# A four-layer graph network on one core: layer 2's table rows come from VectorE products, and its variances, deviations and messages go in two halves

## The chip, the cores and the metric

The kernel runs on one core of a Trainium2 chip. The core has five engines with instruction queues of their own: TensorE (PE in the profile, its weight loads PEld), VectorE (DVE), ScalarE (ACT), GpSimd (POOL) and SyncE (SP), which issues all DMAs here. The engines meet only through semaphores. The metric is the device time of one launch in microseconds. The kernel before takes 3417.18 us, the median of three runs (3413.88 to 3422.05).

## The reference

There are 64 independent graphs of 256 nodes with 128 features, and a sparse 256 x 256 weight matrix `adj` for each. Four layers follow one another; each first normalises its input and cuts it at zero, and adds its result to its input. The change lies in layer 2, which forms a message for every pair of nodes:

```
h   = relu(layernorm(x))
pre[i, j] = h[j] @ W1[:D] + h[i] @ W1[D:] + b1
msg[i, j] = gelu(layernorm(pre[i, j], g1, be1))
agg[i]    = sum over j of adj[i, j] * msg[i, j]
x = x + layernorm(concat(h, agg) @ W2 + b2, g2, be2)
```

Most entries of `adj` are zero, so most messages need not be formed.

## The kernel before

**Blocks and lanes.** A graph's 256 targets i are cut into 8 blocks of 32 (`NIB`, `IB`), its 256 sources j into 3 blocks of 86 (`NJB`, `JB`), which gives 24 blocks (`NT`). In each block the nonzero entries are numbered into at most 128 lanes (`CAP`). For each block t a one-hot matrix `hot[:, t, :]` of 128 rows and 128 lanes is made: rows 0 to 85 choose the source of the lane, row 86 (`JB`) is left for something else, rows 96 to 127 choose the target (`ROWS` is 96). A matmul of `hot[:, t, :]` with a matrix that holds a row for each source and each target then gives, for every lane, the sum of its source's row and its target's row.

**Two such matrices.** `entries` holds for every block the adjacency, the products and the squared lengths that make up the variances; `table` holds `near` (the sources' rows, already multiplied by g1, with b1g = b1 * g1 added) in rows 0 to 85 and `far` (the targets' rows) in rows 96 to 127. Row 86 of `table` is be1, and row 86 of `hot` gets the standard deviation of each lane, so that the matmul gives d * g1 + std * be1; multiplied by 1/std this is the normalised message. W1 and b1 have had their mean taken off in the setup, so the rows need none taken off.

**Layer 2 of one graph**, the generator `layer2` (L1122), in its order:

- `turned`, `near_squares` (L1147), `far_squares` (L1160): TensorE multiplies h by W1's halves into PSUM; ScalarE squares and sums the rows of the result (`a2`, `c2`). Then the graph passes from part "layer2" to "pairs".
- `sums` and `far` fill `entries`; `adjacent` (L1225) copies the adjacency into it by DMA, 96 rows per source block.
- Four groups `entries_of` (L1273) of six blocks each (`TE`): 24 matmuls of `hot` and `entries`; VectorE forms the weights `wgt` and the variances `var`.
- Beside them run `diagonal` (L1173, the messages of a node to itself, two chunks of 128 nodes in one bank), `sources` (L1186) and `targets` (L1208). These multiply h once more, now by `w1g` = W1 * g1, add b1g on VectorE (`near`) or copy on ScalarE (`far`), wait until the messages of the graph before have read the table (`gathered`), and fill the table: three DMAs from `near`, four from `far`.
- Then, once for all 24 blocks: VectorE clamps the variances; ScalarE takes Ln, then Exp twice, for the deviations `std` and their inverses `rs`; TensorE transposes `std`, ScalarE copies it (`stdT`), and a DMA writes it into row 86 of `hot` (L1311).
- Six `block_sums(c, j)` (L1329), the source block j outside and the half c of the targets inside: four matmuls of `hot` and `table`, a VectorE product with `rs`, Gelu on ScalarE, four matmuls that sum the messages by target in the PSUM tile `pagg`. `own_messages` does the same for the diagonal.

**The order of the work.** All layers of all graphs are Python generators, and a planner (`run`, L1453) steps them one at a time. Its `Clock` holds an assumed cost for every instruction and DMA, the time at which each engine comes free, and the last writers and readers of every tile. Among the steps that could begin soonest it takes the one most overdue: graph n is due at 53 us times n (`PERIOD`), less the time that the rest of a graph has taken from that point. Each engine receives its instructions in the order so chosen, so one changed step can move those behind it. Switching ScalarE between the function set that has Ln and Exp and the one that has Gelu and Tanh costs a preload (L117 in the profile), and the planner holds such a step back by 1 us (`SETL`). The dictionary `behind` says how many graphs may stand in each part. `together` and `begun` start several generators beside one another. Where TensorE's queue would be empty for long, `keep_warm` (L180) adds matmuls into an unused half of `pagg` (L189 in the profile). Nearly all other instructions have L267, the planner's issuing line.

**The start.** Lines 423 to 645 hold the setup. `products` (L466) forms `b1g` and `w1g` among others. The generator `fold`, which uses the table's room and is due before everything else, multiplies layer 3's weights; only after its last step may graph 0's table be filled. All loads stand in SyncE's queue in the order of the program.

Of the kernel before, what the change touches and what calls it, by code (L numbers as in the profile page):

```python
# [9 lines left out]
AF = mybir.ActivationFunctionType  # L10
ALU = mybir.AluOpType
AX = mybir.AxisListType
# [12 lines left out]
ROWS = P - IB  # L25
NT = NIB * NJB
NF = NC * NJB
# [244 lines left out]
class Sparse:  # L272
# [150 lines left out]
    def setup(self):  # L423
# [3 lines left out]
        self.ones = self.full("ones", [P, P], 1.0)  # L427
# [151 lines left out]
    def setup_lanes(self):  # L579
# [7 lines left out]
        for c in range(NC):  # L587
# [8 lines left out]
        lane1 = self.c("lane1", [P, CAP])  # L596
        incl = lane1
        nc.gpsimd.affine_select(
            out=incl, in_=self.ones, pattern=[[1, P]], compare_op=ALU.is_ge, fill=0.0, base=0, channel_multiplier=-1
# [20 lines left out]
        nc.gpsimd.iota(lane1, [[1, CAP]], base=1, channel_multiplier=0, **iota)  # L620
        nc.vector.memset(lane1[P - IB :], 1.0)
# [16 lines left out]
        self.near = self.c("near", [ROWS, NJB, D])  # L638
        nc.gpsimd.memset(self.near, 0.0)
        be1 = self.w["L2_gnn_be1"].rearrange("(o n d) -> o n d", o=1, n=1).broadcast_to([1, NJB, D])  # L640
        nc.sync.dma_start(out=self.near[JB : JB + 1], in_=be1)
# [480 lines left out]
    def layer2(self, n, g):  # L1122
# [9 lines left out]
        t2 = self.t("t2", [P, N])  # L1132
        a2 = self.t("a2", [P, NJB])
        c2 = self.t("c2", [P, NC])
        var = self.t("var", [P, NT + NC])
        table, entries = self.table, self.entries

# [9 lines left out]
        def near_squares():  # L1147
# [5 lines left out]
            for j in range(NJB):  # L1153
                w = self.width(j)
                self.squares(a2[:w, j : j + 1], pa[:w, j, :])
                yield
            self.close(self.ps)
            yield

        def far_squares():  # L1160
# [8 lines left out]
            yield  # L1169
            self.close(self.ps)  # L1170
            yield

        def diagonal():  # L1173
            po = yield from self.bank(self.ps, (P, NC, D))
            for c in range(NC):
                self.mm(po[:, c, :], [(hT[:, c * P : (c + 1) * P], self.w1own)])
            yield
            nc.vector.tensor_tensor(own, po, self.over(self.b1, NC), ALU.add)
# [3 lines left out]
            for c in range(NC):  # L1182
                self.squares(var[:, NT + c : NT + c + 1], own[:, c, :])
                yield

        def sources():  # L1186
# [12 lines left out]
            yield  # L1199
            self.close(self.ps)  # L1200
            for j in range(NJB):
                while self.gathered[j] < NC * n or not self.folded:
                    yield
                near = a[:, j].rearrange("p (o d) -> p o d", o=1).to_broadcast([ROWS, NIB, D])
                nc.sync.dma_start(out=table[:ROWS, j], in_=near)
                yield

        def targets():  # L1208
            pc = yield from self.bank(self.ps, (P, NC, D))
            for c in range(NC):  # L1210
# [4 lines left out]
            yield  # L1215
            self.close(self.ps)
            while min(self.gathered) < NC * n or not self.folded:
                yield
            for q in range(NQ):
                of = self.over(far, NJB)[q * IB : (q + 1) * IB]  # L1220
# [4 lines left out]
        def adjacent():  # L1225
            while self.looked < NT // TE * n:
                yield
            for j in range(NJB):
                at, end = j * JB, min(j * JB + ROWS, N)
# [12 lines left out]
        yield from self.together(n, [turned(), near_squares(), far_squares()])  # L1242
        yield from self.enter(n, "layer2", "pairs")
# [29 lines left out]
        def entries_of(t0):  # L1273
# [14 lines left out]
            nc.vector.tensor_reduce(var[:, t0 : t0 + TE], own2, AX.X, ALU.add)  # L1288
            self.give("own2")
            yield  # L1290

        filled = self.begun(n, [sources(), targets()])
        yield from self.together(n, [entries_of(t0) for t0 in range(0, NT, TE)] + [diagonal()])
        rs = self.t("rs2", [P, NT + NC])
        nc.vector.tensor_scalar(rs, var, 0.0, D * LN_EPS, ALU.max, ALU.add)
        yield
        nc.scalar.activation(rs, rs, AF.Ln)
        yield
        std = self.t("std", [P, NT])
        nc.scalar.activation(std, rs[:, :NT], AF.Exp, scale=0.5)  # L1300
        yield
        nc.scalar.activation(rs, rs, AF.Exp, scale=-0.5)
        yield
        pt = yield from self.bank(self.ps, (P, P))
        nc.tensor.transpose(pt[:NT], std, self.ident)
        yield
        stdT = self.t("stdT", [NT, P])
        nc.scalar.copy(stdT, pt[:NT])
        yield
        self.close(self.ps)  # L1310
        nc.sync.dma_start(out=g.hot[JB : JB + 1], in_=stdT)  # L1311
        yield
# [5 lines left out]
        def own_messages():  # L1318
            for c in range(NC):
                nc.vector.scalar_tensor_tensor(  # L1320
                    own[:, c, :], own[:, c, :], rs[:, NT + c : NT + c + 1], self.g1, ALU.mult, ALU.mult
# [7 lines left out]
        def block_sums(c, j):  # L1329

            ts = [(c * NQ + q) * NJB + j for q in range(NQ)]
            yield from self.take("pre")
# [7 lines left out]
            yield from self.messages(pre, m, rs[:, ts[0] : ts[-1] + 1 : NJB])  # L1340
# [13 lines left out]
        yield from self.together(n, [block_sums(c, j) for j in range(NJB) for c in range(NC)] + [own_messages()])  # L1354
# [805 lines left out]
```

## Time and profile before

| | |
|---|---|
| median of 3 runs | 3417.18 us |
| profiled execution | 3408.92 us |
| its span, first to last instruction | 3407.1 us |
| mean granted TensorE clock | 0.971 |
| TensorE busy, keep-warm included | 3110.8 us, 91% |
| keep-warm matmuls | 2074, 291.7 us |
| VectorE busy | 2683.3 us, 79% |
| ScalarE busy | 2288.5 us, 67%; 350 function set loads of 1283 ns in it |
| GpSimd busy | 1317.3 us, 39% |
| one transpose of deviations per graph | first 126.3 us, last 3352.5 us |

Busy time is the union of an engine's instructions. TensorE's matmuls are pipelined and their ends are modelled, so the time between starts says more than the duration. The chain is followed back from the last instruction: at each step to what released it, or to the instruction before it on its engine. A line of groups gives the engine, the operation, the tiles written and read, the shapes, the count, then busy us and the mean ns of one, then the idle time in front of them and what ended it.

### The profile page before, as it was taken

To read this page: it belongs to the slowest core of one execution; us is meant where nothing else is said; L and a number is where in the kernel's file an instruction comes from. 1 tells how busy PE (TensorE), PEld (TensorE's weight loads), DVE (VectorE), ACT (ScalarE), POOL (GpSimd) and SP (SyncE) were. 2 spreads that over 40 slices of the span, in tenths; PEclk is the share of its full clock that TensorE was granted. 3 is DMA by queue.
4 is the path that set the end of the run, shared out by engine and by line. 5 is a ranking of instruction groups with operands and counts; after the bars stand their busy time and mean duration, and the time that the engine had idled before them with its cause. 6 is when DMAs were issued, how large, how long until landed. Compare 5 with 4: busy or idle time off the path is not lost.

```text
span 3407.1 us, 74541 instructions
## 1 busy us (share of the span) xinstructions
PE 3110.8 (91%) x26043; PEld 2717.1 (80%) x26043; DVE 2683.3 (79%) x9292; ACT 2288.5 (67%) x5983; POOL 1317.3 (39%) x3024
## 2 busy tenths in 40 slices
PE   5898999999999999999899999999999999999798
PEld 3687788888888788788787877887887878888687
DVE  8778888787878788887877788788878887786763
ACT  3676667767776677666666767776766776766562
POOL 3534444434433344333343434434433433443230
PEclk7899999999999999999999999999999999999899
DMA  1221112112212122112122121121211121121110
GB/s 48 59 50 47 40 47 58 48 42 52 53 38 55 34 55 58 39 48 53 34 54 58 33 58 44 43 58 48 56 40 49 38 58 48 39 56 42 37 48 25
DMA packets 387733, 161.02 MB, mean 47 GB/s; under 512 B 158739, under 2 KB 387350, under 8 KB 387350
## 3 DMA queue, kind: packets, MB, share of 16 engines
q1 hardware_dynamic: 387350, 156.18, 18.2%
q8 instruction: 208, 3.41, 0.4%
q14 instruction: 175, 1.43, 0.1%
HBM read 28.19 MB, written 8.39 MB: 11 GB/s over the span
## 4 chain that ended last, share of the span: by engine, by line
PE 56%; DVE 23%; ACT 14%; issue 4%; POOL 3%; DMA 1%; DVEq 0%; SPq 0%; ACTq 0%; POOLq 0%
PE bank L267 53%; ACT junka L267 3%; ACT L117 3%; DVE hot L267 2%; DVE agg L267 2%; DVE pos L267 2%; DVE lg L267 1%; ACT h L267 1%; PE pagg L267 1%; DVE rank L267 1%; ACT lg L267 1%; PE pagg L189 1%; DVE held L267 1%; DVE msg L267 1%; POOL lnrs L267 1%
## 5 line engine op out<-in xcount | busy, mean ns | idle before, releaser
L117 ACT ACT_TABLE_LOAD x350 | 449.1, 1283 | 5.8
L267 PE MATMUL bank<-table,hot 128*128 128x128 f32 x3072 | 377.0, 278 | 29.4 <-DMA hot<-stdT 11.6
L267 PEld LDWEIGHTS bank<-table,hot 128*128 128x128 f32 x3072 | 360.8, 193 | 44.8 <-issue 15.5
L267 PE MATMUL bank<-entries,hot 128*128 128x65 f32 x3072 | 358.6, 274 | 0.3 <-DVE near L267 0.2
L267 PEld LDWEIGHTS bank<-entries,hot 128*128 128x128 f32 x3072 | 356.6, 193 | 2.1 <-PE bank L267 0.3
L267 PE MATMUL bank<-wsd,f 128*128 128x256 f32 x1280 | 331.7, 390 | 25.2 <-ACT f L267 20.2
L267 DVE TENSOR_TENSOR msg<-bank,rs 128x512 f32<-128x512 f32 x384 | 256.6, 682 | 81.7 <-PE bank L267 78.9
L189 PE MATMUL pagg<-off,identb 128*128 128x256 bf16 x2074 | 291.7, 279 | 0.3 <-DVE agg L267 0.3
L267 ACT ACTIVATE msg<-msg 128x512 f32<-128x512 f32 x384 | 231.1, 625 | 87.7 <-DVE msg L267 85.7
L267 PEld LDWEIGHTS bank<-wsd,f 128*128 128x128 f32 x1280 | 232.4, 193 | 65.3 <-ACT f L267 32.7
L267 DVE TENSOR_TENSOR hot<-bank,lane 128x384 f32<-128x384 f32 x512 | 261.1, 545 | 18.7 <-PE bank L267 18.1
L267 DVE TENSOR_TENSOR sd<-bank,bsd 128x512 f32<-128x512 f32 x256 | 175.1, 684 | 111.8 <-PE bank L267 110.0
L267 ACT ACTIVATE h<-x,lnnb,lnrs 128x128 f32<-128x128 f32 x384 | 172.0, 485 | 123.6 <-DVE lnnb L267 118.5
L267 PE MATMUL bank<-adjT,sd 128*128 128x256 f32 x768 | 232.8, 385 | 2.7 <-DVE sd L267 2.3
L189 PEld LDWEIGHTS <-identb 128*128 128x128 bf16 x2074 | 202.3, 101 | 39.1 <-issue 2.7
L267 PE MATMUL bank<-adj,sd 128*128 128x256 f32 x768 | 229.9, 381 | 0.0
L267 POOL TENSOR_SCALAR lnrs<-lnmv 128x2 f32<-128x2 f32 x256 | 76.3, 298 | 339.1 <-DVE lnmv L267 304.3
L267 POOL TENSOR_TENSOR lnrs<-lnrs,mhalf 128x2 f32<-128x2 f32 x256 | 193.7, 757 | 21.3
L267 PEld LDWEIGHTS bank<-adjT,sd 128*128 128x128 f32 x768 | 146.0, 192 | 29.2 <-DVE sd L267 4.7
L267 PEld LDWEIGHTS bank<-adj,sd 128*128 128x128 f32 x768 | 147.4, 192 | 20.5
L267 PE MATMUL bank<-w,hT 128*128 128x128 f32 (+2 forms) x896 | 150.2, 286 | 2.8 <-ACT tgt L267 0.9
L267 POOL TENSOR_TENSOR adjT<-adjT,binv 128x512 f32<-128x512 f32 x64 | 83.1, 1299 | 178.4 <-ACT binv L267 173.3
(267 smaller groups left out, 8484.0 us busy)
## 6 DMA issues: line engine op xcount, KB each, us to landing
table<-near SPq DMA_DIRECT2D x192, 384.0 KB
table<-far SPq DMA_DIRECT2D x256, 96.0 KB
adj<-in_adj_dram SPq DMA_DIRECT2D x64, 256.0 KB
x<-in_x_dram SPq DMA_DIRECT2D x64, 128.0 KB
out_dram<-f SPq DMA_DIRECT2D x64, 128.0 KB
entries<-adjT SPq DMA_DIRECT2D x64, 96.0 KB
entries<-adjT SPq DMA_DIRECT2D x64, 84.0 KB
entries<-adjT SPq DMA_DIRECT2D x64, 54.0 KB
```

Source lines behind the costliest of these rows:

```text
L117: self.tc.keep_in_program_order(self.nc.scalar.preload_act_table_set(self.set))
L189: self.nc.tensor.matmul(out, lhsT=lhsT, rhs=rhs, start=False, stop=False, skip_group_check=True)
L267: return c.tc.keep_in_program_order(f(*args, **kw))
```

## The change

- `near_squares` multiplies its PSUM result by g1 on VectorE into `near`, in two operations, after the squares and before the bank is released; `far_squares` likewise into `away` (the tile `far`). The second multiplication of h and `w1g` are gone. `near` exists twice, for even and odd graphs, `far` too.
- The bias is added by the matmul: `lane1`, against which the one-hot matrix is compared, is 0 in row 95, so row 95 of `hot` is 1 in every lane, and row 95 of `near` holds b1g, written by six DMAs in the setup. The adjacency's copy stops at 90 rows per source block (`LOOK`), so that row 95 of `entries` stays 0.
- `sources` and `targets` hold only the waits and the DMAs, and begin before the passage to "pairs".
- The clamp, Ln, Exp, transpose, copy and DMA of the deviations are done for the first and the second half of the target blocks by themselves (`half`), each with its two groups of entries and its chunk of the diagonal. The messages go with c outside and j inside: those of the first half begin when its deviations are on their way and all entries have been issued, those of the second after its own.
- To make room in SBUF: `t2` has one buffer, and the constant `ones` is gone.

```diff
+LOOK = 90
+HT = NT // NC
...
-        self.w1g = self.c("w1g", [P, 2, D])
-        nc.vector.tensor_tensor(self.w1g, w1, self.over(g1, 2), ALU.mult)
+        for near in self.near:
+            for j in range(NJB):
+                nc.sync.dma_start(out=near[ROWS - 1 :, j], in_=self.b1g[ROWS - 1 : ROWS])
...
+        nc.gpsimd.affine_select(
+            out=lane1, in_=lane1, pattern=[[0, CAP]], compare_op=ALU.is_ge, fill=0.0, base=ROWS - 2, channel_multiplier=-1
+        )
...
-        t2 = self.t("t2", [P, N])
+        t2 = self.t("t2", [P, N], bufs=1)
...
+        near = self.near[n % 2]
+        away = self.t("far", [P, NC, D])
...
                 self.squares(a2[:w, j : j + 1], pa[:w, j, :])
                 yield
+            for js, w in ((slice(0, NJB - 1), JB), (slice(NJB - 1, NJB), self.width(NJB - 1))):
+                g1 = self.over(self.g1, pa[:, js].shape[1])
+                nc.vector.tensor_tensor(near[:w, js], pa[:w, js], g1[:w], ALU.mult)
+                yield
...
+            nc.vector.tensor_tensor(away, pc[:, :, :D], self.over(self.g1, NC), ALU.mult)
+            yield
...
-        def diagonal():
-            po = yield from self.bank(self.ps, (P, NC, D))
-            for c in range(NC):
-                self.mm(po[:, c, :], [(hT[:, c * P : (c + 1) * P], self.w1own)])
+        def diagonal(c):
+            po = yield from self.bank(self.ps, (P, D))
+            self.mm(po, [(hT[:, c * P : (c + 1) * P], self.w1own)])
...
         def sources():
-
-            pa = yield from self.bank(self.ps, (P, NJB, D))
-            for j in range(NJB):
-                w = self.width(j)
-                self.mm(pa[:w, j, :], [(hT[:, j * JB : j * JB + w], self.w1g[:, 0, :])])
-            yield
-            a = self.near
-            w = self.width(NJB - 1)
-            b1 = self.over(self.b1g, NJB)
-            nc.vector.tensor_tensor(a[:JB, : NJB - 1], pa[:JB, : NJB - 1], b1[:JB, : NJB - 1], ALU.add)
-            yield
-            nc.vector.tensor_tensor(a[:w, NJB - 1], pa[:w, NJB - 1], self.b1g[:w], ALU.add)
-            yield
-            self.close(self.ps)
             for j in range(NJB):
                 while self.gathered[j] < NC * n or not self.folded:
                     yield
...
         def targets():
-            pc = yield from self.bank(self.ps, (P, NC, D))
-            for c in range(NC):
-                self.mm(pc[:, c, :], [(hT[:, c * P : (c + 1) * P], self.w1g[:, 1, :])])
-            yield
-            far = self.t("far", [P, NC * D], bufs=1)
-            nc.scalar.copy(far, pc.rearrange("p c d -> p (c d)"))
-            yield
-            self.close(self.ps)
...
         yield from self.together(n, [turned(), near_squares(), far_squares()])
+        filled = self.begun(n, [sources(), targets()])
         yield from self.enter(n, "layer2", "pairs")
...
+        def half(c):
+            groups = [entries_of(t0) for t0 in range(c * HT, (c + 1) * HT, TE)]
+            yield from self.together(n, groups + [diagonal(c)])
+            nc.vector.tensor_scalar(rs[:, c], var[:, c], 0.0, D * LN_EPS, ALU.max, ALU.add)
+            yield
+            nc.scalar.activation(rs[:, c], rs[:, c], AF.Ln)
+            yield
+            std = self.t("std", [P, HT])
+            nc.scalar.activation(std, rs[:, c, :HT], AF.Exp, scale=0.5)
+            yield
+            nc.scalar.activation(rs[:, c], rs[:, c], AF.Exp, scale=-0.5)
+            yield
+            pt = yield from self.bank(self.ps, (P, P))
+            nc.tensor.transpose(pt[:HT], std, self.ident)
+            yield
+            stdT = self.t("stdT", [HT, P])
+            nc.scalar.copy(stdT, pt[:HT])
+            yield
+            self.close(self.ps)
+            nc.sync.dma_start(out=g.hot[JB : JB + 1, c * HT : (c + 1) * HT], in_=stdT)
+            yield
+
+        halves = [self.begun(n, [half(c)]) for c in range(NC)]
+        yield from halves[0]
+        while self.looked < NT // TE * (n + 1):
+            yield
         yield from filled
         yield from self.enter(n, "pairs", "messages")
...
-        yield from self.together(n, [block_sums(c, j) for j in range(NJB) for c in range(NC)] + [own_messages()])
+        sums = self.begun(n, [block_sums(0, j) for j in range(NJB)])
+        yield from halves[1]
+        yield from self.together(n, [block_sums(1, j) for j in range(NJB)] + [own_messages()])
+        yield from sums
```

More of the change, by code (lines that the diff above doesn't have):

```diff
@@ L426, in setup @@
         make_identity(self.tc.nc, self.ident)
-        self.ones = self.full("ones", [P, P], 1.0)
         self.half = self.full("half", [P, 2 * NC], 0.5)
@@ L594, in setup_lanes @@
         nc.vector.memset(self.anew[:, 0::JB], 0.0)
-        lane1 = self.c("lane1", [P, CAP])
+        lane1 = self.full("lane1", [P, CAP], 1.0)
         incl = lane1
         nc.gpsimd.affine_select(
-            out=incl, in_=self.ones, pattern=[[1, P]], compare_op=ALU.is_ge, fill=0.0, base=0, channel_multiplier=-1
+            out=incl, in_=incl, pattern=[[1, P]], compare_op=ALU.is_ge, fill=0.0, base=0, channel_multiplier=-1
         )
@@ L637, in setup_lanes @@
         self.table = self.c("table", [P, NJB, NIB, D])
-        self.near = self.c("near", [ROWS, NJB, D])
-        nc.gpsimd.memset(self.near, 0.0)
         be1 = self.w["L2_gnn_be1"].rearrange("(o n d) -> o n d", o=1, n=1).broadcast_to([1, NJB, D])
-        nc.sync.dma_start(out=self.near[JB : JB + 1], in_=be1)
+        self.near = []
+        for n in range(2):
+            near = self.c(f"near{n}", [ROWS, NJB, D])
+            nc.gpsimd.memset(near, 0.0)
+            nc.sync.dma_start(out=near[JB : JB + 1], in_=be1)
+            self.near.append(near)
         self.folded = False
@@ L1131, in layer2 @@
         own = self.t("mown", [P, NC, D])
-        t2 = self.t("t2", [P, N])
+        t2 = self.t("t2", [P, N], bufs=1)
         a2 = self.t("a2", [P, NJB])
         c2 = self.t("c2", [P, NC])
-        var = self.t("var", [P, NT + NC])
+        var = self.t("var", [P, NC, HT + 1])
+        rs = self.t("rs2", [P, NC, HT + 1])
         table, entries = self.table, self.entries
+        near = self.near[n % 2]
+        away = self.t("far", [P, NC, D])
         def turned():
@@ L1169, in far_squares @@
             yield
-            self.close(self.ps)
-            yield
-        def diagonal():
-            po = yield from self.bank(self.ps, (P, NC, D))
-            for c in range(NC):
-                self.mm(po[:, c, :], [(hT[:, c * P : (c + 1) * P], self.w1own)])
-            yield
-            nc.vector.tensor_tensor(own, po, self.over(self.b1, NC), ALU.add)
+            nc.vector.tensor_tensor(away, pc[:, :, :D], self.over(self.g1, NC), ALU.mult)
             yield
@@ L1181, in diagonal, with sources @@
             yield
-            for c in range(NC):
-                self.squares(var[:, NT + c : NT + c + 1], own[:, c, :])
-                yield
-        def sources():
-            pa = yield from self.bank(self.ps, (P, NJB, D))
-            for j in range(NJB):
-                w = self.width(j)
-                self.mm(pa[:w, j, :], [(hT[:, j * JB : j * JB + w], self.w1g[:, 0, :])])
-            yield
-            a = self.near
-            w = self.width(NJB - 1)
-            b1 = self.over(self.b1g, NJB)
-            nc.vector.tensor_tensor(a[:JB, : NJB - 1], pa[:JB, : NJB - 1], b1[:JB, : NJB - 1], ALU.add)
-            yield
-            nc.vector.tensor_tensor(a[:w, NJB - 1], pa[:w, NJB - 1], self.b1g[:w], ALU.add)
+        def diagonal(c):
+            po = yield from self.bank(self.ps, (P, D))
+            self.mm(po, [(hT[:, c * P : (c + 1) * P], self.w1own)])
+            yield
+            nc.vector.tensor_tensor(own[:, c], po, self.b1, ALU.add)
             yield
             self.close(self.ps)
+            yield
+            self.squares(var[:, c, HT:], own[:, c])
+            yield
+        def sources():
             for j in range(NJB):
@@ L1203, in sources @@
                     yield
-                near = a[:, j].rearrange("p (o d) -> p o d", o=1).to_broadcast([ROWS, NIB, D])
-                nc.sync.dma_start(out=table[:ROWS, j], in_=near)
+                of = near[:, j].rearrange("p (o d) -> p o d", o=1).to_broadcast([ROWS, NIB, D])
+                nc.sync.dma_start(out=table[:ROWS, j], in_=of)
                 yield
         def targets():
-            pc = yield from self.bank(self.ps, (P, NC, D))
-            for c in range(NC):
-                self.mm(pc[:, c, :], [(hT[:, c * P : (c + 1) * P], self.w1g[:, 1, :])])
-            yield
-            far = self.t("far", [P, NC * D], bufs=1)
-            nc.scalar.copy(far, pc.rearrange("p c d -> p (c d)"))
-            yield
-            self.close(self.ps)
             while min(self.gathered) < NC * n or not self.folded:
@@ L1219, in targets @@
             for q in range(NQ):
-                of = self.over(far, NJB)[q * IB : (q + 1) * IB]
+                of = self.over(away.rearrange("p c d -> p (c d)"), NJB)[q * IB : (q + 1) * IB]
                 rows = table[ROWS:, :, q * NC : (q + 1) * NC].rearrange("p j c d -> p j (c d)")
@@ L1228, in adjacent @@
             for j in range(NJB):
-                at, end = j * JB, min(j * JB + ROWS, N)
+                at, end = j * JB, min(j * JB + LOOK, N)
                 while at < end:
@@ L1287, in entries_of @@
             self.close(self.ps)
-            nc.vector.tensor_reduce(var[:, t0 : t0 + TE], own2, AX.X, ALU.add)
+            c, t = divmod(t0, HT)
+            nc.vector.tensor_reduce(var[:, c, t : t + TE], own2, AX.X, ALU.add)
             self.give("own2")
             yield
[L1292 to L1312, printed above, removed]
+        def half(c):
[22 more added lines that the diff above has]
+        while self.looked < NT // TE * (n + 1):
+            yield
         yield from filled
@@ L1320, in own_messages @@
                 nc.vector.scalar_tensor_tensor(
-                    own[:, c, :], own[:, c, :], rs[:, NT + c : NT + c + 1], self.g1, ALU.mult, ALU.mult
+                    own[:, c, :], own[:, c, :], rs[:, c, HT:], self.g1, ALU.mult, ALU.mult
                 )
@@ L1331, in block_sums @@
             ts = [(c * NQ + q) * NJB + j for q in range(NQ)]
+            scale = rs[:, c, j:HT:NJB]
             yield from self.take("pre")
@@ L1339, in block_sums @@
             m = self.t("msg", [P, TB, D], bufs=MSGS)
-            yield from self.messages(pre, m, rs[:, ts[0] : ts[-1] + 1 : NJB])
+            yield from self.messages(pre, m, scale)
             g.sums += 1
```

## The prediction

> **What bounds the kernel now.** I read first the page's busy times and its chain (who carries the end), then the busy times of five equal stretches in the middle (steady state or not), then the groups that the change touches, and last one graph's passage through layer 2 in order of time.
>
> ```profile
> PE 3110.8 (91%) x26043; PEld 2717.1 (80%) x26043; DVE 2683.3 (79%) x9292; ACT 2288.5 (67%) x5983; POOL 1317.3 (39%) x3024
> PE 56%; DVE 23%; ACT 14%; issue 4%; POOL 3%; DMA 1%; DVEq 0%; SPq 0%; ACTq 0%; POOLq 0%
> ```
>
> TensorE carries over half of the chain, VectorE a quarter, ScalarE a seventh. None of them is full. Of TensorE's 3110.8 us, 291.7 are the planner's keep-warm matmuls (the group at L189, 2074 of them), so its real work is 2819 us, or 44.0 per graph; VectorE has 41.9 and ScalarE 35.8 per graph.
>
> ```profile
> 1640.00:2160.00 520.00, 477.10 (x4052) 413.20 (x4050) 418.86 (x1437) 358.55 (x950) 204.67 (x471) 0.99 0.19 48
> sum 2600.00, PE 2408.27 PEld 2107.23 DVE 2081.66 ACT 1797.97 POOL 1028.64; mean PE 481.65 PEld 421.45 DVE 416.33 ACT 359.59 POOL 205.73
> ```
>
> Columns: stretch, length, then busy us of PE, weight loads, DVE, ACT, POOL; granted clock, DMA share, GB/s. The five stretches are alike (VectorE 80%, ScalarE 69%), so one price per graph will do. The graph's period is read from the one transpose of deviations that each graph has: its first starts at 126.3 us, its 64th at 3352.5, so 3226.2 / 63 = 51.2 us. DMA moves little and is nowhere near a bound.
>
> ```profile
> L117 ACT ACT_TABLE_LOAD x350 | 449.1, 1283 | 5.8
> L267 ACT ACTIVATE rs<-rs 128x26 f32<-128x26 f32 x128 | 28.8, 225 | 30.6 <-DVE rs L267 28.3
> L267 DVE TENSOR_TENSOR near<-bank,b1g 86x256 f32<-86x256 f32 x64 | 26.7, 417 | 14.7 <-PE bank L267 13.9
> L267 DVE TENSOR_TENSOR mown<-bank,b 128x256 f32<-128x256 f32 x64 | 26.5, 414 | 3.5 <-PE bank L267 3.5
> L267 ACT COPY far<-bank 128x256 f32<-128x256 f32 x64 | 23.4, 365 | 38.0 <-PE bank L267 38.0
> L267 DVE TENSOR_TENSOR near<-bank,b1g 84x128 f32<-84x128 f32 x64 | 17.7, 277 | 0.0
> L267 ACT COPY stdT<-bank 24x128 f32<-24x128 f32 x64 | 15.9, 248 | 10.4 <-PE bank L267 9.5
> ```
>
> These are the durations that I use (busy us, mean ns of one, idle before it and why).
>
> ```profile
> 1710.48 1.29 PEld L267 LDWEIGHTS bank<-w1g,hT 128*86 128x86 f32 x10
> 1711.68 1.42 PEld L267 LDWEIGHTS bank<-entries,hot 128*128 128x128 f32 x12
> ...
> 1731.04 0.28 PE L267 MATMUL bank<-ident,std 128*24 128x128 f32 x1 [0.98 <-ACT std L267]
> 1731.16 0.60 PE L189 MATMUL pagg<-off,identb 128*128 128x256 bf16 x4
> ...
> 1731.94 0.83 SPq L267 DMA_DIRECT2D hot<-stdT  x1
> 1732.04 1.36 PE L189 MATMUL pagg<-off,identb 128*128 128x256 bf16 x11
> ...
> 1734.30 2.92 PE L267 MATMUL bank<-table,hot 128*128 128x128 f32 x24 [0.90 <-issue]
> ...
> 1737.47 0.37 ACT L267 COPY hT<-bank 128x256 f32<-128x256 f32 x1
> 1737.86 1.28 ACT L117 ACT_TABLE_LOAD   x1
> 1739.15 2.19 ACT L267 ACTIVATE msg<-msg 128x512 f32<-128x512 f32 x4
> ```
>
> Three things are seen. The ten weight loads of the second table product hold TensorE from 1710.48 to 1711.68, 1.20 us. From the transpose of the deviations (1731.04) to the first message matmul (1734.30) pass 3.26 us in which TensorE mostly runs 15 keep-warm matmuls: the deviations go to SBUF, then by DMA into their row, 2.36 us from issue to the matmul. And a switch of ScalarE's function set costs 1.29 us from instruction to instruction.
>
> **The price of an engine's microsecond.** Work taken from an engine shortens the time only where that engine lies on the chain. Chain share of the period over the engine's work: TensorE 0.56 x 51.2 / 44.0 = 0.65, VectorE 0.23 x 51.2 / 41.9 = 0.28, ScalarE 0.14 x 51.2 / 35.8 = 0.20 us of time per us of work.
>
> **Part one: the table rows from the products of the squares.**
> The ten matmul instructions with w1g go: -1.20 us of TensorE. Two of its PSUM banks per graph go too; that I count at nothing, since their holding is some 2 us of 51.
> The two near operations are the same shapes from the same PSUM layout, a product by g1 in place of the sum with b1g: 0.
> The far copy leaves ScalarE, -0.365, and becomes a VectorE product of 256 columns out of PSUM: +0.414, by the mown row.
> The bias goes through the one-hot matrix (a 1 in row 95, the bias row in near): no instruction per graph.
> The copy of the adjacency moves 90 rows rather than 96 in two of three blocks: 0, its DMAs are issued at 1732.81 for entries that are read at 1755.
> The products by g1 now stand in series ahead of "pairs", 0.69 + 0.41 us of VectorE and its queue, where before they ran beside the entries; against that TensorE no longer has 1.20 us of w1g matmuls in front of the entries. Bounds -1.2 (only that) to +3 us of latency (each waits for a few 0.4 to 0.7 us operations of others); graphs overlap, so I take +0.1 of the period.
> The seven fill DMAs (three near, four far) move ahead of the entries on SyncE's queue, by up to 8 us; between 1700 and 1711.99 the queue issued nothing, so they pass no other DMA there. They were issued at 1711.99 to 1720.4 and needed at 1734.30, so earlier gains nothing; SyncE waits in order, and a fill that waits for its product holds the queue by the 1 us of that product: 0, and the 14 us of lead hides it. If that lead were gone, a late fill would delay the message matmuls by its full wait.
> In the setup SyncE gains six 512-byte DMAs of the bias row, each some 0.45 us, behind VectorE's b1g, which ends at 20.17; the loads behind them go from 13.08 (the first fold matrix) to about 24.9, 12 us later. The fold ends in a memset at 133.1 and graph 0's first fill follows at 135.8, its messages at 142.4, though its deviations left at 126.9. So the fold is what graph 0 waits for. Bounds 0 (SyncE stood still anyway from 21.5 to 29.3 and 30.6 to 42.3) to 12; I take +5 once, nearer the lower since the stalls are longer than the delay.
>
> **Part two: two halves.**
> TensorE: one more transpose, whose row shows 0.12 us to the next start (1731.04 to 1731.16). The diagonal's matmuls are the same ones in two banks. Net of TensorE with part one: -1.08.
> VectorE: the diagonal sum becomes two of 128 columns, 2 x 0.277 - 0.414 = +0.14; the clamp of the variances, 0.178 in its row, is done twice: +0.17. With part one +0.73.
> ScalarE: one more Ln (0.225), two more Exp (0.222 and 0.225), one more copy (0.248), less the far copy: +0.56.
> SyncE: one more 0.82 us issue of deviations; SyncE is idle there: 0.
> Function sets: before, 350 / 64 = 5.5 loads per graph. The last variance of the half that comes first ends at 1716.1, of the second at 1718.92; the Ln came at 1730.14, right behind a load. Where the set is still Gelu's, both halves wait and then go together: no load more. Where the first goes at once and a Tanh or Gelu gets between, it is two more. Bounds -0.2 (a reshuffle) to +2; I take +0.5, that is 0.64 us. On the chain lie 3% of 3407 us, 102 of the 449 us of loads, 0.23 of each us: +0.15.
> The wait of 3.26 us: half 0's messages can start some 2.8 us earlier (1718.92 - 1716.1), and half 1's wait lies beside half 0's 24 message matmuls (2.8 us). Bounds: nothing (the first half waits for the set like the second) to 2.8 us; I take half a microsecond of TensorE's empty time, x 0.65 = -0.3.
>
> The Trainium skill speaks against the halves here: ScalarE: Activation LUTs, "What ACT_TABLE_LOAD costs", has a load of about 1.28 us and a drain of about 1.38 us, 2.66 us for every switch. This trace agrees with the load alone: Copy at 1737.47, load at 1737.86, Gelu at 1739.15. By the page, half a load more would be an estimated 1.33 us of ScalarE and +0.31 of the period in place of +0.15, 10 us on the total.
>
> **Sum.** Per graph: TensorE -1.08 x 0.65 = -0.70; VectorE 0.73 x 0.28 = +0.20; ScalarE 0.56 x 0.20 = +0.11; loads +0.15; the wait -0.30; the front +0.10. Together -0.44, x 63 periods = -28; setup +5: -23 us. The profiled execution took 3408.9 us (span 3407.1), so 3386; the median shown, 3417.2, is 8.3 above it, so 3394.
>
> **Rivals.**
> 1. Set switches decide, slower. Half 1's Ln comes after a Gelu of half 0 or a Tanh of another graph in every graph: two loads more. In the chain between 1700 and 1760 three of the six loads lie on it, so at half of 1.283 each: +1.28 x 63 = +81, and -0.59 x 63 + 5 = -32 from the rest: 3408.9 + 49 + 8.3 = 3466. It decides from 32 / 63 / 0.64 = 0.8 load more per graph on. For it: the halves are ready 2.8 us apart, and after 1700 the loads start only 7.4 to 18.0 us apart. Against: the planner charges a switch with 1 us.
> 2. TensorE is the bound after all: 1.08 counts in full, VectorE and ScalarE hide theirs. -68 - 19 + 5: 3335. For it: 91% busy with the keep-warm. Against: 33 keep-warm matmuls per graph (1649 in 2600 us), which stand where TensorE has no work.
> 3. VectorE becomes the bound: 0.73 counts in full, TensorE's gain is taken up by keep-warm matmuls, +0.26 of ScalarE stays: 46 + 16 + 5: 3484. For it: 80% busy, and three more steps in layer 2's series wait in its queue. Against: 23% of the chain.
> 4. Nothing that shows: TensorE's gain becomes keep-warm time and the rest cancels: 3417.
>
> **How the numbers follow.** 0.2% is 7 us, about what a measurement here can tell from no change. Chances: the forecast 0.45 (its own range 3370 to 3415), TensorE 0.13, nothing 0.09, set switches 0.20, VectorE 0.13. Faster: 0.45 less its edge, and 0.13: 0.56. The same: 0.10. Slower: 0.34. The range reaches to rival 2's value below and just past rival 1's above: 3335 to 3468, leaving out half of rivals 2 and 3.
>
> **What would show it.** The profile after should have no w1g group, 128 transposes of 12 columns, some 380 table loads, a TensorE real work near 42.9 us per graph, keep-warm matmuls about as many as before, VectorE near 42.6, and message matmuls of the first half that start before the second half's deviations are out. Over 430 loads would speak for rival 1, a busier VectorE with more keep-warm matmuls for rival 3. A first message matmul later than 150 us would show that the setup's queue costs more than 5. The planner writes the order from modelled times, so every changed step moves all choices behind it; if that reshuffle is worth more than 1%, I am wrong for a cause that no step above holds.

## The result, and the profile after

The changed kernel takes 3432.36 us (median of 12 runs, 3424.52 to 3446.43), beside 3412.74 us for the kernel before in the same comparison (12 runs). The ratio is 1.0063, with a 95% interval of 1.0048 to 1.0079: 20 us slower, where 23 us less was forecast. The profiled execution took 3428.59 us, its span 3426.9 us.

The page of the kernel after, its busy times and its chain:

```profile
PE 3100.0 (90%) x25492; PEld 2690.5 (79%) x25492; DVE 2714.4 (79%) x9483; ACT 2360.1 (69%) x6215; POOL 1316.9 (38%) x3026
PE 54%; DVE 25%; ACT 12%; issue 4%; POOL 4%; DMA 1%; SPq 0%; DVEq 0%; ACTq 0%; POOLq 0%
```

The engines did what was forecast of them: VectorE 42.4 us per graph (2714.4 / 64), ScalarE 36.9, and TensorE has 551 matmuls fewer. Yet TensorE's busy time falls by 11 us only. The same stretch, 600 to 3200 us, as one window of the kernel after, and then of the kernel before (columns as in the prediction: the granted clock is the third figure from the end):

```profile
600.00:3200.00 2600.00, 2391.48 (x19753) 2074.39 (x19752) 2109.12 (x7340) 1856.51 (x4873) 1016.84 (x2353) 0.96 0.19 47
```

```profile
600.00:3200.00 2600.00, 2408.27 (x20290) 2107.23 (x20289) 2081.66 (x7163) 1797.97 (x4706) 1028.64 (x2358) 0.98 0.19 47
```

The clock fell from 0.98 to 0.96. In the trace's clock records it has two values, 1.0 and 0.5. Added up over the whole execution, TensorE stood at half clock for 203 us before and for 289 us after (mean clocks 0.971 and 0.958). The added time lies in this middle stretch, 113 us before and 201 after.

The groups of the kernel after that answer to those shown of before:

```profile
L119 ACT ACT_TABLE_LOAD x390 | 500.4, 1283 | 6.4
L269 ACT ACTIVATE rs<-rs 128x13 f32<-128x13 f32 x256 | 49.9, 210 | 28.5 <-DVE rs L269 25.2
L269 DVE TENSOR_TENSOR mown<-bank,b 128x128 f32<-128x128 f32 x128 | 34.6, 281 | 1.3 <-PE bank L269 1.2
L269 ACT COPY stdT<-bank 12x128 f32<-12x128 f32 x128 | 29.2, 249 | 29.5 <-PE bank L269 28.3
L269 DVE TENSOR_TENSOR near<-bank,g 86x256 f32<-86x256 f32 x64 | 26.7, 418 | 62.9 <-ACT junka L269 62.6
L269 DVE TENSOR_TENSOR far<-bank,g 128x256 f32<-128x256 f32 x64 | 26.4, 412 | 0.0
```

Every duration lies within 0.02 us of the one that the prediction used. One thing is new: VectorE is idle for 62.9 us in front of `near`, about 1 us per graph, and what ends the wait is ScalarE's sum of squares (`junka`), because the product now stands behind the squares.

One graph's passage (graph 31), in order of time:

```profile
1718.97 1.55 PE L269 MATMUL bank<-entries,hot 128*128 128x65 f32 x12 [0.89 <-DVE sd L269]
...
1727.28 0.21 ACT L269 ACTIVATE std<-rs 128x12 f32<-128x12 f32 x1
...
1731.12 1.45 PE L269 MATMUL bank<-entries,hot 128*128 128x65 f32 x12
...
1732.41 0.27 PE L269 MATMUL bank<-ident,std 128*12 128x128 f32 x1
...
1732.72 0.25 ACT L269 COPY stdT<-bank 12x128 f32<-12x128 f32 x1 [3.51 <-PE bank L269]
...
1733.00 4.82 SPq L269 DMA_DIRECT2D hot<-stdT  x2
...
1733.26 1.59 PE L191 MATMUL pagg<-off,identb 128*128 128x256 bf16 x13
...
1735.11 1.13 PE L269 MATMUL bank<-table,hot 128*128 128x128 f32 x8 [0.26 <-ACT h L269]
```

The first half's deviations are out of ScalarE at 1727.5, but their transpose stands in TensorE's queue behind the last entries of the second half and starts at 1732.41, 4.9 us later. From there to the first message matmul, at 1735.11, TensorE again runs 13 keep-warm matmuls. (The line of SyncE holds both halves' DMAs; the second is issued at 1737.0.) The wait that the halves were to shorten is still there: averaged over graphs 8 to 61 it is 4.05 us from the first transpose to the first message matmul, where it was 3.99. In 60 of the 64 graphs the first half's transpose stands behind all entries.

The start, SyncE's issues:

```profile
12.92 0.43 SPq L269 DMA_DIRECT2D be<-in_L_gnn_be_dram  x1
21.94 3.77 SPq L269 DMA_DIRECT2D near<-b1g  x6
25.75 0.58 SPq L269 DMA_DIRECT2D w<-in_L_gnn_W_dram  x1
...
27.83 0.43 SPq L269 DMA_DIRECT2D table<-in_L_gnn_wu_dram  x1
```

and the load of the first fold matrix in the kernel before:

```profile
13.08 0.43 SPq L267 DMA_DIRECT2D table<-in_L_gnn_wu_dram  x1
```

The queue stands still from 13.4 to 21.9 us until b1g is there; the first fold matrix is fetched at 27.83 where it was 13.08. Graph 0's first message matmul comes at 179.1 us where it was 142.4. Its output leaves at 256.8 (205.0 before), that of graph 10 at 752.8 (730.3), that of graph 63 at 3422.7 (3401.9). From graph 10 to graph 63 a graph takes 50.38 us where it took 50.41: no gain per graph. The 22 us at graph 10 are not simply what is left of the 52 at graph 0: the output of graph 3 comes only 7 us later (383.1, 375.8 before), so most of the late start is made up by then, and the lag grows again behind it.

### The profile page after: what moved, and what is told of

Read it like the earlier page. It is cut to its first block, busy times and chain, and to the rows that moved or that the text cites. A ratio compares the mean times of both kernels' runs of the same rounds, so it can differ in the third digit from the quotient of the medians.

```text
span 3426.9 us, 74183 instructions
## 1 busy us (share of the span) xinstructions
PE 3100.0 (90%) x25492; PEld 2690.5 (79%) x25492; DVE 2714.4 (79%) x9483; ACT 2360.1 (69%) x6215; POOL 1316.9 (38%) x3026
## 4 chain that ended last, share of the span: by engine, by line
PE 54%; DVE 25%; ACT 12%; issue 4%; POOL 4%; DMA 1%; SPq 0%; DVEq 0%; ACTq 0%; POOLq 0%
PE bank L269 52%; ACT junka L269 3%; DVE hot L269 2%; DVE pos L269 2%; ACT L119 2%; DVE agg L269 2%; DVE held L269 1%; DVE lg L269 1%; PE pagg L269 1%; DVE rank L269 1%; PE pagg L191 1%; ACT h L269 1%; POOL lnrs L269 1%; DVE msg L269 1%; DVE sd L269 1%
## 5 line engine op out<-in xcount | busy, mean ns | idle before, releaser
L269 PE MATMUL bank<-entries,hot 128*128 128x65 f32 x3072 | 379.5, 280 | 8.6 <-ACT entries L269 3.8
L269 PEld LDWEIGHTS bank<-entries,hot 128*128 128x128 f32 x3072 | 373.2, 199 | 16.0 <-ACT entries L269 5.9
L191 PE MATMUL pagg<-off,identb 128*128 128x256 bf16 x2099 | 300.5, 280 | 0.0
L269 ACT ACTIVATE z<-z 128x512 f32<-128x512 f32 x192 | 119.9, 624 | 53.2 <-DVE z L269 51.4
```

Of the source, the lines that this page charges most:

```text
L191: self.nc.tensor.matmul(out, lhsT=lhsT, rhs=rhs, start=False, stop=False, skip_group_check=True)
L269: return c.tc.keep_in_program_order(f(*args, **kw))
```

## The experiments

Two theories stood at first. A: the work of the engines decides, as in the prediction, and the six bias DMAs in the setup add to it; then undoing one or the other gives its price back, within some 5 us. R: the order that the planner writes decides; then any edit, even one that changes none of the work, moves the time by as much as the whole change does. A third, C, came from the clock records: gaps in TensorE's work hold its clock at half for longer.

All results. "Half" is the time at half clock, worked out from the clock records of the profiled run; "first" is the start of graph 0's first message matmul. The kernel before lay between 3409.6 and 3413.4 us in these comparisons. Each median is of 4 to 12 runs, but for after_r (2), before_r and after_s (3 each).

| run | median us | ratio (95%) | clock | half us | first us |
|---|---|---|---|---|---|
| before | 3412.7 | 1 | 0.971 | 203 | 142.4 |
| after | 3432.4 | 1.0063 (1.0048 to 1.0079) | 0.958 | 289 | 179.1 |
| late_bias | 3390.1 | 0.9940 (0.9927 to 0.9953) | 0.964 | 244 | 151.8 |
| setup_only | 3419.9 | 1.0027 (1.0013 to 1.0042) | 0.965 | 244 | 175.3 |
| rows_only | 3374.2 | 0.9895 (0.9881 to 0.9910) | 0.968 | 219 | 141.4 |
| rows_early | 3389.4 | 0.9930 (0.9909 to 0.9951) | 0.970 | 209 | 180.4 |
| halves_only | 3421.8 | 1.0031 (1.0018 to 1.0043) | 0.966 | 233 | 142.1 |
| before_p | 3430.6 | 1.0058 (1.0041 to 1.0075) | 0.958 | 288 | 143.9 |
| after_p | 3409.9 | 0.9998 (0.9987 to 1.0009) | 0.959 | 280 | 180.0 |
| late_p | 3437.1 | 1.0076 (1.0064 to 1.0089) | 0.951 | 337 | 152.6 |
| before_q | 3477.6 | 1.0189 (1.0167 to 1.0211) | 0.970 | 211 | 143.5 |
| after_q | 3413.2 | 1.0000 (0.9987 to 1.0013) | 0.956 | 305 | 180.4 |
| before_r | 3426.2 | 1.0048 (1.0030 to 1.0066) | 0.965 | 243 | 142.1 |
| after_r | 3435.6 | 1.0072 (1.0044 to 1.0100) | 0.960 | 278 | 178.9 |
| before_s | 3416.0 | 1.0014 (0.9990 to 1.0038) | 0.962 | 262 | 142.6 |
| after_s | 3433.6 | 1.0067 (1.0040 to 1.0094) | 0.964 | 247 | 179.0 |
| before_warm | 3402.3 | 0.9979 (0.9967 to 0.9990) | 0.982 | 125 | 141.9 |
| after_warm | 3410.7 | 1.0000 (0.9989 to 1.0010) | 0.971 | 201 | 178.9 |
| late_p_warm | 3392.2 | 0.9952 (0.9934 to 0.9970) | 0.975 | 169 | 153.5 |
| rows_only_warm | 3367.2 | 0.9876 (0.9862 to 0.9889) | 0.972 | 191 | 141.5 |

### The setup's queue: late_bias and setup_only

`late_bias` is the changed kernel with its six DMAs moved to the end of `fold`:

```diff
         nc.vector.tensor_tensor(self.b1g, b1, g1, ALU.mult)
-        for near in self.near:
-            for j in range(NJB):
-                nc.sync.dma_start(out=near[ROWS - 1 :, j], in_=self.b1g[ROWS - 1 : ROWS])
...
+        for near in self.near:
+            for j in range(NJB):
+                nc.sync.dma_start(out=near[ROWS - 1 :, j], in_=self.b1g[ROWS - 1 : ROWS])
+        yield
```

> The changed kernel with the six bias-row DMAs moved from the setup to the end of the fold, so that no load stands behind them on SyncE. Theory A (the setup's queue): the changed kernel loses its 20 us in the start alone; graph 0's first message matmul went from 142.4 to 179.1 us and the period after graph 10 is the same 50.4 us, so this one should be back at graph 0 near 145 us and take 3413 us, 20 below the changed kernel and level with the kernel before. Theory B (the steady part is worse, by the 40 added function set loads and the lower granted clock, 0.958 against 0.971): moving six DMAs gives at most the first few us, 3425 to 3432.

`setup_only` is the kernel before with only those DMAs:

```diff
         nc.vector.tensor_tensor(self.b1g, b1, g1, ALU.mult)
+        for _ in range(2):
+            for j in range(NJB):
+                nc.sync.dma_start(out=self.near[ROWS - 1 :, j], in_=self.b1g[ROWS - 1 : ROWS])
```

> The kernel before with nothing but six bias-row DMAs behind b1g in the setup (the row is multiplied by zeros there). Theory A: the loads of the fold go from 13.1 to about 28 us, graph 0's first message matmul to 170 us or later, and the time to 3433, as in the changed kernel. Theory B: the start's delay is made up by the graphs behind it, 3413 to 3418.

That the six DMAs delay the first message is shown both ways: 179.1 us becomes 151.8 with them behind the fold, 142.4 becomes 175.3 with them alone. What this costs at the end is not the same in the two: 42 us in the changed kernel, 8 us in the kernel before. A delay of 33 us that costs 8 in one order and 42 in another is not a price of the setup; the rest of the 42 is likely what the moved start does to the order behind it, which these two runs alone do not show.

### One part alone: rows_only, rows_early and halves_only

`rows_only` has part one (late bias), and layer 2 in one piece as before:

```diff
-        def half(c):
-            groups = [entries_of(t0) for t0 in range(c * HT, (c + 1) * HT, TE)]
-            yield from self.together(n, groups + [diagonal(c)])
...
+        yield from self.together(n, [entries_of(t0) for t0 in range(0, NT, TE)] + [diagonal()])
+        rs = self.t("rs2", [P, NT + NC])
```

> Part one alone: table rows by VectorE, bias through the matmul, one pass of deviations and messages as before; the bias-row DMAs at the end of the fold. If TensorE's freed 1.20 us per graph counts at the price of the prediction: -0.78 + 0.12 + 0.10 - 0.07 = -0.63 us per graph, 40 us below the kernel before, 3373. If the freed time only lowers the granted clock and fills with keep-warm matmuls: 3405 to 3420.

`halves_only` is part two on the kernel before (the same lines the other way round, with `sources` and `targets` as they were):

```diff
-        yield from self.together(n, [entries_of(t0) for t0 in range(0, NT, TE)] + [diagonal()])
-        rs = self.t("rs2", [P, NT + NC])
...
+        halves = [self.begun(n, [half(c)]) for c in range(NC)]
+        yield from halves[0]
+        while self.looked < NT // TE * (n + 1):
+            yield
```

> Part two alone: the kernel before with deviations and messages in halves; the setup as before. By the prediction's terms: loads +0.15, the wait -0.30, VectorE +0.09, ScalarE +0.18, TensorE +0.08: +0.2 us per graph, 3425. If the wait ahead of the messages is worth its 2.8 us: 3340. If the function sets decide: over 380 loads and 3440 or more.

`rows_early` is `rows_only` with the bias DMAs in the setup, as the change has them:

```diff
+        for near in self.near:
+            for j in range(NJB):
+                nc.sync.dma_start(out=near[ROWS - 1 :, j], in_=self.b1g[ROWS - 1 : ROWS])
...
-        for near in self.near:
-            for j in range(NJB):
-                nc.sync.dma_start(out=near[ROWS - 1 :, j], in_=self.b1g[ROWS - 1 : ROWS])
-        yield
```

> Part one alone with the six bias-row DMAs in the setup, as the change has them, against part one alone with them at the end of the fold (3374.2). Theory A: some 42 us above, 3416, with graph 0's first message matmul near 175 us. Theory R: 8 to 20 us above, 3382 to 3394, since the delayed start is partly made up and the rest of the 42 was the order.

Part one alone is 37 us faster than before, and with its DMAs early still 21 us; part two alone is 10 us slower, with 32 function set loads more. At 3374.2 us `rows_only` lies on the 3373 that the prediction's own prices gave for it. On these runs alone one would say that the rows pay and the halves cost. The next group shows how far that can be trusted.

### The order alone: other due times

The kernels p, q, r and s differ from theirs in one constant, the due time between two graphs, which adds or removes no operation of the kernel's work; the planner's choices move with it, and with them keep-warm matmuls and set loads:

```diff
-PERIOD = 53.0
+PERIOD = 53.2
```

(53.2 in p, 52.8 in q, 52.6 in r, 53.4 in s; `late_p` is `late_bias` with 53.2.)

> The kernel before with the planner's due time of 53.2 us per graph in place of 53.0; no other edit. It measures what a reshuffle of the order alone is worth. Theory R (much of what these changes show is reshuffle): the time moves by 10 us or more, either way. Theory A (the setup's queue and the engines' work decide): within 5 us of 3411.5.

> The changed kernel with the due time of 53.2 us; no other edit. Theory A: within 5 us of 3432. Theory R: moved by 10 us or more, likely downward, since the changed kernel was then an unlucky order; 3405 to 3422.

> The changed kernel with the bias-row DMAs at the end of the fold, at the due time of 53.2 us. Theory A: 3390 within 5 us, and 42 below the changed kernel at the same due time. Theory R: 10 us or more away from 3390, and the setup's share, changed kernel less this one at the same due time, is nearer the 8 us that it cost in the kernel before.

> The kernel before at the due time of 52.8 us, nothing else edited. Theory R (reshuffle of the order is worth 10 to 40 us): anywhere from 3390 to 3440, at least 8 us from 3411. Theory A (the edits' own work decides): within 5 us of 3411, and 53.2 was an exception.

> The changed kernel at the due time of 52.8 us, nothing else edited. Theory R: 3395 to 3445; the difference to the kernel before at the same due time may have either sign. Theory A: 3432 within 5 us.

> The kernel before at the due time of 52.6 us. Theory R: anywhere from 3400 to 3480. Theory A: 3411 within 5.

> The changed kernel at the due time of 52.6 us. If the change is worth what the prediction's steady terms said, 28 us a run less 10 for the setup, it is below the kernel before at the same due time in most of the five pairs and by some 20 us in the mean; if it is worth nothing, the signs are mixed and the mean lies within the spread.

> The kernel before at the due time of 53.4 us. Theory R: 3400 to 3480, not within 5 us of the 3411 at 53.0. Theory A: 3411 within 5.

> The changed kernel at the due time of 53.4 us. With an effect of its own of some -18 us: 5 to 60 us below the kernel before at the same due time. With none: either sign, and the mean of the five pairs within 20 us of zero.

The kernel before goes from 3413 to 3431, 3478, 3426 and 3416 us; the kernel after from 3432 to 3410, 3413, 3436 and 3434; `late_bias` from 3390 to 3437. Five of the nine moves are 18 us or more, about as large as the result itself. Beside 53.0, the difference after minus before is therefore +19.6, -20.7, -64.4, +9.4 and +17.7 us at the five due times: a mean of -8, with a standard deviation of 36 and so a standard error of 16. Over five orders the kernel before has a mean of 3433, the kernel after 3425. The bias DMAs early instead of late, which cost 42 us at 53.0, gain 27 us at 53.2. Put side by side, ScalarE's instructions of `before` and `before_p` come in the same order for the first 639 of 5983 and part there; those of `after` and `after_p` part after 546 of 6215. Theory A has no room for any of this, theory R does, though three of its own statements missed: `before_q` lies above its 3440, `before_s` within 5 us of 3411, and the setup's share at 53.2 is -27, not near 8.

Where an order costs, it need not be by the clock. `before_q`, the cores' view and the window:

```profile
core 0: 3475.5 us, clock 0.970
```

```profile
600.00:3200.00 2600.00, 2418.61 (x20152) 2097.71 (x20154) 2040.72 (x7064) 1799.16 (x4635) 1007.10 (x2333) 0.98 0.18 47
```

It is 65 us slower than `before` at the same clock, and VectorE does 41 us less work in the same 2600 us. A graph stays longer under way: from layer 2's first matmul to its sums 66.8 us, against 51.6 in `before`. (This counts up to the transpose of the sums.) The trace shows the step. The last message matmul ends 49.1 us after layer 2's first matmul in both kernels, but VectorE reads the sums (`agg`) 15.7 us after that, where it was 0.3; the diagonal's messages, its other input, are done earlier still. What kept the planner from placing that reading sooner was not followed.

### The clock alone: the same order, the gaps filled

To test C, `keep_warm` was made to issue more matmuls into a gap than the planner counts, from 100 us on, so that the order stays as it was:

```diff
+        more = int((gap - 0.1) / 0.12) if gap > 0.25 and begin > 100 else 0
...
-        for _ in range(n):
+        for _ in range(more):
...
-            self.fed += rhs.shape[1]
+        self.fed += n * rhs.shape[1]
```

> The changed kernel with the late bias rows at the due time of 53.2 us (3437.1 us, granted clock 0.951, 337 us of it at half clock), with more keep-warm matmuls in the same gaps of TensorE; the planner does not count the added ones, so all other instructions stand in the same order. Theory C (an order costs time through the stretches of half clock that it leaves): the granted clock goes to 0.97 or more and the time to 3400 to 3415. Theory W (the order costs through waits between the engines, and the low clock is only their shadow): the clock rises, the time stays within 5 us of 3437, or rises, since the added matmuls stand in front of real ones.

> The kernel before (granted clock 0.971, 203 us at half clock) with the same added keep-warm matmuls, order kept. Theory C: 0.3 to 0.5 us per us of half clock removed, 3370 to 3395. Theory W: 3411 or more.

> The changed kernel with more keep-warm matmuls in the same gaps, order kept (it has 289 us at half clock, a granted clock of 0.958). Theory C (the loss is the half clock): back to 3390 to 3412, as 3437 went to 3392 in the other order. Theory W (the loss is waits in the start and between engines): 3420 to 3435, as the kernel before gained only 9 us.

> Part one alone, bias rows late, with more keep-warm matmuls, order kept: 3374.2 without them, 219 us at half clock. Theory C: 0.2 to 0.5 us per us of half clock that goes, some 90 us of it, 3330 to 3357. Theory W: 3365 to 3375.

In all four pairs the streams of VectorE, ScalarE, GpSimd and SyncE are the same, instruction for instruction, in the filled kernel, and TensorE has the same matmuls apart from the keep-warm, in the same order but for 6 to 42 places in the trace. The core, the window and the keep-warm group of `late_p`:

```profile
core 0: 3436.0 us, clock 0.951
```

```profile
600.00:3200.00 2600.00, 2401.73 (x19648) 2095.36 (x19647) 2079.30 (x7265) 1804.40 (x4807) 1009.87 (x2341) 0.95 0.19 47
```

```profile
L191 PE MATMUL pagg<-off,identb 128*128 128x256 bf16 x2101 | 293.7, 278 | 0.0
```

and the same three views of `late_p_warm`:

```profile
core 0: 3387.0 us, clock 0.975
```

```profile
600.00:3200.00 2600.00, 2456.49 (x20805) 2149.57 (x20806) 2112.17 (x7404) 1840.41 (x4907) 1030.56 (x2379) 0.98 0.19 48
```

```profile
L192 PE MATMUL pagg<-off,identb 128*128 128x256 bf16 x3080 | 415.2, 276 | 0.3 <-DVE agg L270 0.3
```

979 matmuls more, whose result nobody reads, bring the clock from 0.951 to 0.975, and in the same 2600 us VectorE gets 33 us more of its work done. The time falls by 45 us. Since the order is the same, this is what the half clock that came of those gaps had cost.

A price for it can be worked out afterwards: if of each microsecond at half clock half is lost, and TensorE's share of the chain of that reaches the end, then `late_p` 168 us less at half clock x 0.5 x 0.53 = 45 (measured 45); `after` 88 x 0.5 x 0.54 = 24 (22); `rows_only` 28 x 0.5 x 0.49 = 7 (7); `before` 78 x 0.5 x 0.56 = 22 (7, beside its own comparison's 3409.6). Three of four fit; the kernel before gains less. Of theory C's ranges only that of `after_warm` was met: `late_p_warm` fell further, `before_warm` and `rows_only_warm` less, and the last lies in the range of theory W.

The views of `after_warm`, in which the changed kernel stands at the clock of the kernel before, and then the core of `before_warm`:

```profile
core 0: 3413.9 us, clock 0.971
```

```profile
600.00:3200.00 2600.00, 2449.41 (x20654) 2134.95 (x20652) 2115.56 (x7356) 1869.41 (x4892) 1028.70 (x2361) 0.98 0.19 47
```

```profile
core 0: 3395.4 us, clock 0.982
```

The gain of the filling comes in the steady part: the output of graph 10 of `after_warm` leaves at 752.2 us (752.8 in `after`), and from there a graph takes 50.13 us for 50.38.

A second sign needs no edit. One and the same kernel has a slightly different clock in each execution: over 86 runs of the kernel before in these comparisons it lies between 0.966 and 0.978, and the time rises by 0.24 us per us at half clock worked out from it (correlation 0.73), about the 0.25 to 0.27 of the three that fit.

`rows_only_warm` is the fastest kernel of the study: 3367.24 us, 0.9876 of before (0.9862 to 0.9889).

## Why the prediction was wrong

**The step that failed** is the conversion in "the price of an engine's microsecond": it turned 1.08 us less of TensorE's work into 0.70 us less time per graph, as if the order behind the change and the clock stayed as they were. The period did not move (50.41 to 50.38 from graph 10 on), while the time at half clock rose from 203 to 289 us; with it back at 201, in the same order, the period is 50.13 and the time 22 us less. The prediction's last sentence names the cause that no step of it holds, a reshuffle worth more than 1%, and put no term and no chance on it; the due times show that in the kernel before it is worth from 3 to 65 us.

**TensorE, -1.08 per graph.** The matmuls went: 23969 to 23393 without the keep-warm, 9 per graph. But TensorE's real work, its busy time less the keep-warm, fell from 2819.1 to 2799.5 us, 0.3 per graph. The 86 us more at half clock can lengthen matmuls by up to 43 us, most of what is missing of 69. On the end they are worth 86 x 0.5 x 0.54 = 23 us by the rule above. That agrees with `after_warm`: with its gaps filled until the clock is that of before (0.971), the changed kernel takes 3410.7, the time of the kernel before. Filling the gaps of the kernel before as well takes it to 3402.3, so filled against filled the change is still some 8 us slower, with 201 us at half clock beside 125. Whether the added half clock belongs to the change or to its order is not shown: over the five due times the kernel before has 203 to 288 us of it (mean 241), the kernel after 247 to 305 (mean 280).

**VectorE, ScalarE.** Right in size: 42.4 us per graph for 42.6, 36.9 for 37.0 (35.8 + 0.56 + 0.64). What they cost at the end was not measured apart.

**Function set loads.** 390 for 380: +0.62 per graph for +0.5. Rival 1 needed over 430 and did not come; nor did rival 3, whose mark was more keep-warm matmuls (2099 for 2074). Rivals 2 and 4 forecast no loss.

**The wait, -0.30, and the front, +0.10.** Averaged over graphs 8 to 61, the first message matmul follows the first entry after 17.1 us where it was 19.4: 2.3 us earlier, by the halves (17.5 in `halves_only`, 19.3 in `rows_only`). But the entries follow layer 2's first matmul after 15.2 us where it was 12.6: 2.6 us later, near the upper bound of 3. That `near` and `far` in series alone cause it is not shown: `rows_only`, which has them in series too, has 12.9. Together the two nearly cancel; from layer 2's first matmul to the transpose of the sums a graph takes 52.9 us for 51.6. Both signs hold in all five pairs of due times, with means of 1.5 us earlier and 2.8 us later. The half microsecond of TensorE's empty time that the prediction took did not show in the wait behind the transpose (4.05 us for 3.99): the first half's transpose stands behind the second half's entries. The prediction's term left out that the messages wait by construction until all entries are issued, so that a first half that is ready early can't bring its messages ahead of the second half's entries.

**The setup, +5.** The mark named for its failure, a first message after 150 us, was passed at 179.1. The first fold matrix moved by 14.75 us, for the 12 that the prediction had as its upper bound, and the first message by 37, which the prediction did not follow through the fold. At the end, the kernel before shows 8 us for it (`setup_only`) and part one alone 15 (`rows_early`), around that bound; in the two pairs of the whole change it is 42 and -27, and cannot be told from the order. Up to graph 10 the four pairs agree better: its output leaves 17, 20, 28 and 31 us later with the DMAs early. So +5 was likely too little, but the five orders of the kernel before alone spread that output from 728.5 to 772.6 us.

**What stays open.** The forecast -23 and the measured +20 lie 43 us apart. 22 of these are the clock, as `after_warm` measures it. The other 21 can't be given to a step: changes of order alone spread by a standard deviation of 26 us in the kernel before and 12 in the kernel after. Whether the change is good apart from its order is not settled either: -8 us with a standard error of 16 over five pairs. That the rows alone are good is likely (3374 and 3389 lie below all five orders of the kernel before) but was seen at one due time only. And why the planner holds back the reading of the sums in `before_q` was not followed.

## What to carry to other kernels

Where a planner writes the order, one build is one draw: move a constant that changes no work, time both kernels at several values, and believe no difference smaller than that spread. Work taken from TensorE may be no gain where the clock falls in the gaps, so read the granted clock beside the busy time, and try filling the gaps without letting the planner count the filling. A DMA that waits for a result holds the loads behind it on its queue: six rows of 512 bytes, early instead of late or absent, moved the first message by 27 to 39 us in four pairs.

## What the runs showed of the hardware

Added matmuls that do no work shorten the time: 979 of them by 45 us, 1020 by 22 us, and 1003 and 969 by 7 us each.

The half clock comes in stretches of 3.41 us and multiples of it (20 of the 44 in the profile after are one such stretch, 14 are two). On that grid of 3.41 us, in the kernel before, 31 windows at full clock were followed by a drop: TensorE was busy for a median of 47% of them. 897 were not followed by one, and 99% of these were busy for 60% or more. But 10 of the 31 were too, so the busy share of that one window does not decide alone. A gap of the window's whole length is not needed: the longest gap in the 3.41 us ahead of a drop has a median of 1.15 us. The Trainium skill, TensorE: Matmul & The Clock Gate, "What's actually happening", has the same two states and the same window, and lets the clock fall after at least one idle window. The windows agree with the trace; idle, read as empty, does not, since windows about half busy were enough here.
